# A gated graph layer on one Trainium2 core: edge lists made for 128 targets at once, a mark stored once and loaded twice by ScalarE's queue, constants on VectorE, an evenly paced opening

## The chip, the cores and the metric

The kernel runs on one core of one Trainium2 chip. The metric is the device time of one execution in microseconds (us). A core has five engines, each with a queue of its own that is worked off in order: TensorE (PE; its weight loads are shown as PEld), VectorE (DVE), ScalarE (ACT), GpSimd (POOL) and SyncE (SP). SP, ACT and POOL issue DMAs; what SP issues is shown as queue q1, what ACT issues as q10, POOL's indirect ones as q0. The engines wait for one another through semaphores. SBUF is the working memory, PSUM takes the results of matmuls.

## The reference

There are 16 batches of 1024 nodes with 256 features, and one adjacency matrix of 1024 x 1024 that is almost empty: under 1% of it is not zero. Cut to what matters:

```
pre_u  = h @ W1[:256];  pre_v = h @ W1[256:]
S[u,v] = sigmoid(relu(pre_u[u] + pre_v[v] + b1) @ W2 + b2)
a[v]   = sum over u of S[u,v] * adj[u,v] * h[u]
m[v]   = (sum over u of adj[u,v] * h[u]) * h[v]
out    = beta1*h + beta2*(a @ Wa + ba) + beta3*(m @ Wm + bm)
```

S is needed only where adj is not zero, so the kernel works on lists of edges.

## The kernel before, in words

**Blocks, windows, steps.** Targets v are cut into 8 blocks of 128, batches into 4 groups of 4. One *block* of the main loop is one pair of group and block of targets; there are 32, numbered k, the group g = k // 8. The 128 targets of a block are two *windows* of 64. A window's edges lie in 640 slots, 5 *steps* of 128 edges each. So the main loop has 320 steps n, ten to a block, and s is the step within the block.

**A step.** Five buffers hold fetched rows: `fetch` (line 402) gathers for 128 edges the rows of the sources from `table[g]`, four steps ahead, on POOL; a row holds pre_u and h of four batches. `expand` (413) multiplies the window's *mark*, a 0/1 matrix that says which target each slot belongs to, with the targets' rows X, and so spreads pre_v over the edges; it is called two steps ahead. `gate` (429) adds both on DVE (432), takes relu, the product with W2 and its sum (436), then the sigmoid on ACT (439), and ACT scales the one-hot rows with it (441). `aggregate` (443) sums on PE into 64 targets x 2 kinds (449). After five steps `window_end` (453) copies the sums (456), multiplies by h and transposes; after ten `block_end` (477) multiplies by Wm and Wa (489) and stores.

**The marks.** A mark is 128 x 640 floats: 64 targets, twice, since X holds a high part in one half of the partitions and a low part in the other (`halves`, 308). `lists` makes it, stores all 128 rows to `who` (219), and `load_mark` (409) loads it on SP's queue into one of two buffers, which the main loop calls at line 523, in step 3 and step 8 of each block, for the window whose first `expand` comes at the end of that same step. On SP's queue stand also the loads of `hT` (269) and `h_blk` (521), 512 KB each, and the stores of `tab` (292) and of the result (499).

**The lists.** For each of the 8 blocks of targets `lists` (162) loads 128 rows of the transposed adjacency matrix, finds up to 24 sources of each target with three rounds of max on DVE, counts them, finds by a matmul with a triangular constant at which slot each target begins (187 to 190), and then, window by window (208): marks the slots (215, 217), multiplies the mark with the rows R of the lists (222), copies the result by ACT (226), picks from it on DVE each edge's source (228 to 238) and its one-hot row (239), and gathers the 5 x 128 values of the matrix on POOL (243). It is a generator: each `yield` gives the turn back, and the caller sets the order. In the opening two lists run side by side; lists 4 to 7 are worked on in the main loop, one piece a step (537).

**The rows.** `rows` (272) makes one block of `table[g]` and pv, the targets' pre_v: four pieces of eight matmuls each, in the order u, v, u, v. The pieces share two PSUM buffers ("misc") with much else; u is copied by ACT (290), v by DVE (297) a step later. x itself is copied from DRAM to DRAM on ACT's queue (277). The 8 blocks of group 0 are made in the opening; in groups 0 to 2 the main loop makes those of the next group, 4 or 5 pieces a block.

**The order.** It is written out by hand: the order of the calls is the order in each engine's queue, and `after(step, f)` (259) puts f off to a later step. The opening is the loop of lines 356 to 369: 32 rounds, each with one piece of rows, one piece of each of the two lists that run, and in rounds 5 and on the halves of block 0. Then come the last weights (371 to 377), their scaling on DVE, the first marks and the first five fetches. After step 60, `count_rest` (248) takes on POOL a maximum over all partitions of how many edges did not fit, and DVE reads it at once (252). If any are left, a loop at the end works them off; with these inputs it has nothing to do.

**Constants.** POOL makes them with iota and memset (98 to 117), DVE compares (119 to 132), and POOL clears the five fetch buffers (334).

Of the kernel before, what the change touches and what calls it, by code (L numbers as in the profile page):

```python
# [14 lines left out]
P = 128  # L15
# [3 lines left out]
def kernel(  # L19
# [57 lines left out]
    who = [dram.tile([P, E], FP, name=f"who{w}") for w in range(NT * NW)]  # L77
# [20 lines left out]
    def iota(shape, pattern, base, step, name):  # L98
        t = const.tile(shape, FP, name=name)
        nc.gpsimd.iota(t, pattern=pattern, base=base, channel_multiplier=step,  # L100
                       allow_small_or_imprecise_dtypes=True)
        return t

    ident = const.tile([P, P], FP, name="ident")
    make_identity(nc, ident)
    ones = const.tile([P, 2], FP, name="ones")
    nc.vector.memset(ones[:, 0:1], 1.0)
    nc.vector.memset(ones[:, 1:2], -1.0)
    ukey = const.tile([P, N], FP, name="ukey")
# [3 lines left out]
    slot_of = iota([P, TW], [[P, TW]], 0, 1, "slot_of")  # L113
    nth = iota([P, S], [[1, S]], 0, 0, "nth")
    place = iota([P, W], [[1, W]], 0, 0, "place")
# [4 lines left out]
    nc.vector.tensor_scalar(mine, row_of.rearrange("p w t v -> p w (t v)"), row, None, ALU.is_equal)  # L120
    before = const.tile([P, NW, P], FP, name="before")
    nc.vector.tensor_scalar(before, row_of.rearrange("p w t v -> p w (t v)"), row, None, ALU.is_gt)
    swap = const.tile([P, P], FR, name="swap")
    far = iota([P, NW, W], [[-W, NW], [1, W]], W, 0, "far")
    nc.vector.tensor_scalar(swap, far.rearrange("p w v -> p (w v)"), row, None, ALU.is_equal)
    late = const.tile([P, 1], FP, name="late")
    nc.vector.tensor_scalar(late, row, float(W), None, ALU.is_ge)
    nc.vector.tensor_scalar(before[:, 1, :], before[:, 1, :], late, None, ALU.mult)

    ahead = const.tile([P, NW, W], FP, name="ahead")  # L130
    for w in range(NW):
        nc.vector.tensor_copy(ahead[:, w, :], before[:, w, :W])
# [29 lines left out]
    def lists(vt):  # L162
# [23 lines left out]
        for w in range(NW):  # L186
            nc.tensor.matmul(pw[:, w * RC:(w + 1) * RC], mine[:, w, :], R, start=True, stop=True)
# [485 lines left out]
```

## Time and profile before

| what | us |
|---|---|
| median of three runs (lowest, highest) | 1495.53 (1494.21, 1500.91) |
| the profiled execution | 1498.72 |
| its span in the trace | 1496.9 |
| busy in the span: PE | 1323.4 (88%) |
| busy in the span: VectorE | 1219.2 (81%) |
| busy in the span: ScalarE | 902.8 (60%) |
| busy in the span: GpSimd | 446.5 (30%) |

The profiled execution is one more run, and its own time is 1.8 us more than its span. A row of instructions reads: start, length, engine and line, operation, what is written <- what is read, shape, how many merged (x), and in brackets how long the engine had been idle before it and what ended that. "misc", "pc" and "acc" are PSUM buffers. A row of waits reads: who waited <- for whom, total, times, longest. A group's row has busy time and, behind it, the mean of one in ns. Matmuls are pipelined, so 8 of 0.39 us each that are shown as one row of 1.9 us are usual.

### The profile page before, as it was taken

How to read it: one execution, taken by the hardware profiler on the slowest of the kernel's cores; microseconds unless marked ns; L12 is line 12 of the kernel's file. 1: busy time of each engine (PE TensorE's matmuls, PEld its weight loads, DVE VectorE, ACT ScalarE, POOL GpSimd, SP SyncE). 2: the span in 40 equal slices, each digit the busy share in tenths (PEclk: the TensorE clock that was granted, in tenths of full speed). 3: DMA queues.
4: the chain of work that ended last, by engine and by line, in shares of the span. 5: the costliest groups of instructions: out<-in, count | busy, mean ns of one | idle time of the engine just before them, and what ended most of it. 6: DMA issues, size and time to landing. Idle time of an engine off the chain costs nothing.

```text
span 1496.9 us, 20978 instructions
## 1 busy us (share of the span) xinstructions
PE 1323.4 (88%) x6064; PEld 1118.5 (75%) x6064; DVE 1219.2 (81%) x3521; ACT 902.8 (60%) x2570; POOL 446.5 (30%) x420
## 2 busy tenths in 40 slices
PE   4776788878997979999997979988999999999987
PEld 3555677767786868887886868877888877778876
DVE  7774898879976968876986978867888999999984
ACT  1212564545665757755775757655777777778763
POOL 2543253334522222222222222222222333333320
PEclk8897999989998989999999999999999999999999
DMA  4447768767796879877987878877998898889982
GB/s 133 148 148 276 274 242 290 240 210 270 234 339 218 314 292 327 297 269 267 330 320 267 314 292 316 303 263 262 330 332 311 318 334 320 320 323 322 335 302 70
DMA packets 152396, 414.35 MB, mean 277 GB/s; under 512 B 17120, under 2 KB 100576, under 8 KB 116064
## 3 DMA queue, kind: packets, MB, share of 16 engines
q0 software_dynamic: 48640, 296.70, 55.2%
q1 hardware_dynamic: 84496, 97.86, 18.8%
q10 hardware_dynamic: 19136, 18.35, 3.9%
q8 instruction: 51, 0.84, 0.2%
q14 instruction: 73, 0.60, 0.1%
HBM read 412.99 MB, written 55.57 MB: 313 GB/s over the span
## 4 chain that ended last, share of the span: by engine, by line
PE 45%; DMA 12%; DVE 6%; issue 4%; ACT 1%; POOL 1%; POOLq 0%; SPq 0%; DVEq 0%
PE acc L449 21%; DMA mark<-who 10%; PE misc L489 9%; PE misc L287 7%; PE pc L418 6%; DVE t L436 3%; DVE t L432 2%; PE misc L471 2%; DMA fetched<-table,uidx 2%; POOL fetched L404 1%; PE misc L322 1%; ACT left L441 0%; DVE ev L460 0%; DVE low L314 0%; ACT LT L473 0%
## 5 line engine op out<-in xcount | busy, mean ns | idle before, releaser
L449 PE MATMUL acc<-fetched,left 128*128 128x256 f32 x2560 | 635.6, 393 | 30.5 <-ACT ev L456 18.8
L404 POOL DMA_INDIRECT fetched<-table,uidx x320 | 344.9, 1078 | 928.8 <-PE acc L449 777.5
L449 PEld LDWEIGHTS acc<-fetched,left 128*128 128x128 f32 x2560 | 500.2, 197 | 127.6 <-ACT ev L456 25.7
L436 DVE SCALAR_TENSOR_TENSOR t<-t,w_b 128x256 f32<-128x256 f32 x1280 | 470.3, 422 | 21.8 <-DVE t L432 0.9
L432 DVE TENSOR_TENSOR t<-fetched,pc 128x1024 f32<-128x1024 f32 x320 | 388.5, 1214 | 87.0 <-PE pc L418 62.6
L441 ACT ACTIVATE left<-left,gt 128x64 f32<-128x64 f32 x1280 | 340.9, 337 | 10.4
L418 PE MATMUL pc<-X,mark 128*128 128x512 f32 x640 | 248.3, 470 | 64.9 <-DMA mark<-who 52.6
L439 ACT ACTIVATE gt<-sc,b_b 128x4 f32<-128x4 f32 x320 | 95.9, 300 | 245.2 <-DVE t L436 243.5
L418 PEld LDWEIGHTS pc<-X,mark 128*128 128x128 f32 x640 | 119.8, 197 | 87.0 <-issue 44.3
L426 ACT ACTIVATE left<-onehot,val 128x256 f32<-128x256 bf16 x320 | 157.7, 493 | 5.3 <-DMA w_m<-in_Wm_dram 5.3
L287 PE MATMUL misc<-w_u,hT 128*128 128x256 f32 x512 | 132.3, 404 | 32.2 <-DVE pv L297 19.3
L287 PEld LDWEIGHTS misc<-w_u,hT 128*128 128x128 f32 x512 | 101.5, 202 | 50.8 <-DVE pv L297 21.8
L325 ACT CAST X<-misc 64x512 fp32r<-64x512 f32 x128 | 74.3, 580 | 106.4 <-PE misc L322 105.2
L489 PE MATMUL misc<-w_m,LT 128*128 128x256 f32 x512 | 135.3, 388 | 0.6 <-ACT X L325 0.3
L287 PE MATMUL misc<-w_v,hT 128*128 128x256 f32 x512 | 128.9, 397 | 5.7 <-ACT tab L290 4.1
L489 PE MATMUL misc<-w_a,LT 128*128 128x256 f32 x512 | 131.4, 379 | 0.0
L290 ACT COPY tab<-misc 128x512 f32<-128x512 f32 x64 | 37.5, 585 | 147.4 <-PE misc L287 139.0
L287 PEld LDWEIGHTS misc<-w_v,hT 128*128 128x128 f32 x512 | 99.9, 198 | 23.9 <-ACT tab L290 6.8
L489 PEld LDWEIGHTS misc<-w_m,LT 128*128 128x128 f32 x512 | 99.7, 196 | 16.3 <-ACT X L325 1.0
L243 POOL DMA_INDIRECT val<-in_adjT_dram,vidx x80 | 90.1, 1126 | 69.0 <-DVE none L202 24.0
L489 PEld LDWEIGHTS misc<-w_a,LT 128*128 128x128 f32 x512 | 97.5, 190 | 13.5
L436 DVE DVE_READ_ACCUMULATOR t<-t,w_b 128x1 f32 x1280 | 103.9, 81 | 0.0
(100 smaller groups left out, 933.6 us busy)
## 6 DMA issues: line engine op xcount, KB each, us to landing
mark<-who SPq DMA_DIRECT2D x65, 320.0 KB, 8.7
hT<-in_xT_dram SPq DMA_DIRECT2D x32, 512.0 KB, 11.5
table<-in_x_dram ACTq DMA_DIRECT2D x32, 512.0 KB, 8.5
table<-tab SPq DMA_DIRECT2D x32, 512.0 KB, 6.4
h_blk<-in_x_dram SPq DMA_DIRECT2D x32, 512.0 KB, 12.5
out_dram<-h_blk SPq DMA_DIRECT2D x32, 512.0 KB, 5.4
who<-made SPq DMA_DIRECT2D x16, 320.0 KB, 2.5
fetched<-table,uidx POOLq DMA_INDIRECT x320, 8.0
```

Of the source, the lines that this page charges most:

```text
L243: nc.gpsimd.indirect_dma_start(out=val[:, i, j:j + 1], out_offset=None, in_=adj_flat, in_offset=bass.IndirectOffsetOnAxis(ap=vidx[:, i, j: ...
L287: nc.tensor.matmul(p[:, bb * D:(bb + 1) * D], hT[:, 2 * h + bb, i, :], wt[:, i, :], start=(i == 0), stop=(i == DC - 1))
L325: nc.scalar.copy(X[s, w, c], pl[s])
L404: nc.gpsimd.indirect_dma_start(out=fetched[n % NF], out_offset=None, in_=table[g], in_offset=bass.IndirectOffsetOnAxis(ap=uidx[:, vt * NW ...
L418: nc.tensor.matmul(pcs[n][:, c], marks[n // TW][:, j * P:(j + 1) * P], cuts[k][:, w, c], start=True, stop=True)
L426: nc.scalar.activation(lefts[n][:, :, w, :], onehot[:, i, j, :].unsqueeze(1).to_broadcast([P, GB, W]), AF.Copy, scale=val[:, i, j:j + 1])
L432: nc.vector.tensor_tensor(t, fetched[n % NF][:, :GD].rearrange("p (b d) -> p b d", b=GB), pcs.pop(n).rearrange("p (b d) -> p b d", b=GB), ...
L436: nc.vector.scalar_tensor_tensor(t[:, b, :], t[:, b, :], 0.0, w2_b, ALU.max, ALU.mult, accum_out=sc[:, b:b + 1])
L439: nc.scalar.activation(gt, sc, AF.Sigmoid, bias=b2_b)
L441: nc.scalar.activation(lefts[n][:, b, 1 - w, :], lefts[n][:, b, w, :], AF.Copy, scale=gt[:, b:b + 1])
L449: nc.tensor.matmul(accs[n // TW][:, b, :], left[:, b].rearrange("p k v -> p (k v)"), f[:, GD + b * D:GD + (b + 1) * D], start=(j == 0 and ...
L489: nc.tensor.matmul(pz[:, bb * D:(bb + 1) * D], LTs[k][:, b * DC + c, i, :], wt[:, c, :], start=(i == 0 and c == 0), stop=(i == 1 and c == ...
```

## The change

- **Lists.** Both windows of a block go through one pass: one pair of marking operations for all 128 targets, five matmuls over 128 partitions with two masked copies of R side by side, one copy by ACT, one chain on DVE over 10 columns in place of 5, then all ten gathers. The start of each target's slots comes from one matmul, and DVE reads it from PSUM. A list has 9 pieces, where it had 12.
- **Mark.** `who` holds 64 rows; each load is two DMAs, one for each half of the partitions, issued by ACT. In the main loop they are issued in steps 4 and 9 of a block for the window after the next, behind that step's `gate` and `left_adj`.
- **Constants.** All are made on VectorE from one scan and a 32 x 32 transpose; POOL keeps the clearing of `val` and of the fetch buffers.
- **Rows.** The order is u, u, v, v; in group 0 both v pieces go to the PSUM tile of the sums and are copied in one operation.
- **Opening.** The 36 pieces of lists 0 to 3 are spread evenly over the 32 rounds, the two running lists by turns. The last weights are loaded eight rounds before the end, and are scaled after step 3 of the main loop.
- **Main loop.** No list piece in step 0 or in any step with s = 8. The all-reduce stays after step 60, DVE reads it twelve steps later.

```diff
-    who = [dram.tile([P, E], FP, name=f"who{w}") for w in range(NT * NW)]
+    who = [dram.tile([W, E], FP, name=f"who{w}") for w in range(NT * NW)]
...
-    slot = iota([P, E], [[1, E]], 0, 0, "slot")
...
-    row = iota([P, 1], [[0, 1]], 0, 1, "row")
-    row_of = iota([P, NW, 2, W], [[W, NW], [0, 2], [1, W]], 0, 0, "row_of")
-
-    mine = const.tile([P, NW, P], FP, name="mine")
-    nc.vector.tensor_scalar(mine, row_of.rearrange("p w t v -> p w (t v)"), row, None, ALU.is_equal)
...
+    upto = fixed([P, E], "upto")
+    nc.vector.tensor_scalar(upto, ukey[:, :E], -1.0, float(N), ALU.mult, ALU.add)
+    rows32 = fixed([P, 32], "rows32")
+    nc.vector.transpose(rows32, upto[:, :32])
+    row = rows32[:, 0:1]
...
+    nc.vector.tensor_scalar(ahead[:, :W], upto[:, :W], row, None, ALU.is_gt)
+    nc.vector.tensor_scalar(ahead[:, W:], upto[:, W:P], row, late, ALU.is_gt, ALU.mult)
...
+    slot, nth, place = upto, upto[:, :S], upto[:, :W]
@@ lists
         pw = aside(vt)
-        for w in range(NW):
-            nc.tensor.matmul(pw[:, w * RC:(w + 1) * RC], mine[:, w, :], R, start=True, stop=True)
-        for w in range(NW):
-            nc.tensor.matmul(pw[:, NW * RC + w:NW * RC + w + 1], before[:, w, :], R[:, 0:1], start=True, stop=True)
-        nc.tensor.matmul(pw[:, NW * RC + NW:NW * RC + NW + 1], ahead.rearrange("p w v -> p (w v)"), R[:, 0:1],
-                         start=True, stop=True)
+        nc.tensor.matmul(pw[:, 0:1], ahead, R[:, 0:1], start=True, stop=True)
         yield
-        Rw = wk.tile([P, NW * RC + NW + 1], FP, name="Rw", bufs=2)
-        nc.scalar.copy(Rw, pw[:, :NW * RC + NW + 1])
+        first = R[:, 1:2]
+        nc.vector.tensor_copy(first, pw[:, 0:1])
...
+        early = wk.tile([P, E], FP, name="early", bufs=1)
+        nc.vector.tensor_scalar(early, slot, R[:, 0:1], None, ALU.is_lt)
...
+        mark = big.tile([P, E], FP, name="made", bufs=2)
+        nc.vector.scalar_tensor_tensor(mark, slot, first, early, ALU.is_ge, ALU.mult)
...
-        for w in range(NW):
...
-            mark = big.tile([P, E], FR, name="made", bufs=1)
-            nc.vector.scalar_tensor_tensor(mark, slot, first, early, ALU.is_ge, ALU.mult)
-            yield
-            nc.sync.dma_start(who[i], mark.bitcast(FP))
-            pe = aside(vt)
-            for j in range(TW):
-                nc.tensor.matmul(pe[:, j * RC:(j + 1) * RC], mark[0:W, j * P:(j + 1) * P].bitcast(FP), Rv[0:W, :],
-                                 start=True, stop=True)
-            yield
...
+        yield
+        RR = wk.tile([P, NW, RC], FP, name="RR", bufs=2)
+        for w, mine in enumerate((soon, late)):
+            nc.vector.tensor_scalar(RR[:, w, :], R, mine, None, ALU.mult)
+            nc.sync.dma_start(who[vt * NW + w], mark[w * W:(w + 1) * W])
+        pe = aside(vt)
+        for j in range(TW):
+            nc.tensor.matmul(pe[:, j * NW * RC:(j + 1) * NW * RC], mark[:, j * P:(j + 1) * P],
+                             RR.rearrange("p w r -> p (w r)"), start=True, stop=True)
+        yield
+        M = NW * TW
+        L = wk.tile([P, M, RC], FP, name="L", bufs=2)
+        nc.scalar.copy(L.rearrange("p (w j) r -> p w j r", w=NW),
+                       pe[:, :M * RC].rearrange("p (j w r) -> p w j r", w=NW, r=RC))
...
+        yield
+        nc.vector.tensor_tensor(onehot[:, sl].rearrange("p w j v -> p (w j) v"),
...
+        for i in range(vt * NW, (vt + 1) * NW):
             for j in range(TW):
                 nc.gpsimd.indirect_dma_start(
...
@@ rows
+        for wt in (w_u, w_v):
+            for h in range(2):
+                c = slice(2 * h * D, (2 * h + 2) * D)
+                if wt is w_v and g == 0 and h == 0:
+                    both = psa.tile([P, GD], FP, name="acc")
+                p = both[:, c] if wt is w_v and g == 0 else small("p")
...
+                elif g:
+                    after(step + 1, lambda c=c, p=p: keep(c, p))
+                elif h == 1:
+                    after(step + 1, lambda both=both: keep(slice(0, GD), both))
@@ opening
-    while m < 0 or any(pair):
...
-        for i in range(2):
-            if pair[i] and not (m < 2 - 4 * NT and i == 1) and next(pair[i], 0) == 0:
+    OP = 4 * NT
+    for m in range(OP):
+        all_rows.send(m - OP - 10)
...
+        for _ in range((m + 1) * 9 * EARLY // OP - m * 9 * EARLY // OP):
+            i = at % 2 if pair[at % 2] else (at + 1) % 2
+            at += 1
+            if pair[i] and next(pair[i], 0) == 0:
...
+        if m == OP - 8:
+            w_a = load_weights(Wa, "w_a")
...
+    def scale_late():
...
+    after(3, scale_late)
@@ load_mark
         marks[q] = big.tile([P, E], FR, name="mark")
-        nc.sync.dma_start(marks[q].bitcast(FP), who[q % (NT * NW)])
+        src = who[q % (NT * NW)]
+        for h in range(2):
+            nc.scalar.dma_start(marks[q][h * W:(h + 1) * W].bitcast(FP), src)
@@ main loop
-        if n % TW == TW - 2 and n + TW < total:
-            load_mark(n // TW + 1)
...
+        if n % TW == TW - 1 and n // TW + 2 < total // TW:
+            load_mark(n // TW + 2)
...
-        if n < total:
+        if 0 < n < total and s != 8:
             next(more, None)
...
         if n == 60:
-            count_rest()
+            nc.gpsimd.partition_all_reduce(longest, rest, P, bass_isa.ReduceOp.max)
+            after(n + 12, count_rest)
```

More of the change, by code (lines that the diff above doesn't have):

```diff
@@ L6 @@
 from concourse._compat import with_exitstack
-from concourse.masks import make_identity
 FP = mybir.dt.float32
@@ L246, in lists @@
                     bounds_check=N * N - 1, oob_is_err=False)
+    longest = const.tile([P, NT], FP, name="longest")
     def count_rest():
-        longest = const.tile([P, NT], FP, name="longest")
-        nc.gpsimd.partition_all_reduce(longest, rest, P, bass_isa.ReduceOp.max)
         most = const.tile([P, 1], FP, name="most")
```

137 lines of the change are left out of this document (59 added, 78 removed).

## The prediction

> **What bounds the kernel now.** I read the table by stage first. I cut it at VectorE's add of line 432, which begins each edge step: 140.70 is step 0, and a block of 128 targets is ten steps. Columns: length, then busy time with instruction count of PE, PEld, DVE, ACT and POOL, then granted clock, DMA share and GB/s.
>
> ```profile
> 0.00:140.70 140.70, 91.80 (x390) 72.01 (x390) 88.83 (x215) 24.79 (x46) 59.38 (x64) 0.88 0.51 161
> 140.70:403.60 262.90, 221.47 (x978) 180.80 (x979) 226.59 (x669) 141.84 (x405) 96.20 (x84) 0.92 0.75 258
> 403.60:443.70 40.10, 39.19 (x187) 33.77 (x186) 34.34 (x102) 29.81 (x87) 14.56 (x15) 1.00 0.87 315
> 443.70:493.70 50.00, 41.67 (x184) 35.29 (x183) 34.02 (x103) 25.67 (x73) 11.80 (x11) 0.90 0.72 243
> 493.70:528.60 34.90, 34.90 (x169) 30.30 (x168) 32.68 (x96) 27.04 (x79) 11.15 (x10) 1.00 0.88 320
> 528.60:707.70 179.10, 163.31 (x736) 139.38 (x735) 135.95 (x394) 111.35 (x319) 42.24 (x40) 0.93 0.81 288
> 707.70:785.90 78.20, 77.90 (x375) 67.91 (x374) 68.38 (x197) 57.27 (x165) 21.57 (x20) 1.00 0.92 328
> 785.90:867.80 81.90, 74.25 (x350) 64.40 (x349) 66.76 (x195) 52.62 (x151) 21.64 (x20) 0.96 0.80 287
> 867.80:1046.70 178.90, 159.79 (x736) 137.06 (x735) 135.69 (x395) 111.47 (x319) 42.30 (x40) 0.96 0.80 288
> 1046.70:1197.30 150.60, 150.30 (x723) 131.19 (x722) 135.03 (x393) 109.89 (x316) 42.29 (x40) 1.00 0.91 323
> 1197.30:1437.80 240.50, 225.08 (x1054) 190.42 (x1053) 225.68 (x675) 185.86 (x540) 75.78 (x70) 0.99 0.89 321
> ```
>
> There are five stages. The opening (140.7) keeps PE and DVE each some two thirds busy, so neither bounds it alone. Blocks 0 to 4 (262.9), where four lists are still made, are nearest to DVE (226.6 busy). Blocks that make rows for the next group are bound by PE: at 707.7 two take 78.2 with PE busy for 77.9. The stages at 528.6 and 867.8 are four such blocks each, the same work as twice 78.2 = 156.4, yet take 179.1 and 178.9, with PE idle for 16 to 19 us. The last seven whole blocks are DVE's, 225.7 of 240.5. The idle time of PE is explained by the waits, then SyncE's issues in order of time, then the marks' DMAs.
>
> ```profile
> DVE t L432 <- PE pc L418: 62.6, 31, 8.1
> PE pc L418 <- DMA mark<-who: 52.6, 13, 8.0
> ```
>
> ```profile
> 528.41 0.38 SPq L521 DMA_DIRECT2D h_blk<-in_x_dram  x1
> 528.84 0.96 SPq L269 DMA_DIRECT2D hT<-in_xT_dram  x1
> 529.89 9.51 SPq L411 DMA_DIRECT2D mark<-who  x1
> ```
>
> ```profile
> L411 SPq DMA_DIRECT2D mark<-who x65: 319/373/11349, 125.9 to 1437.9; - x65
> ...
> DMA to landing us min/median/max: 3.6/8.7/22.4
> ```
>
> Line 418 spreads a window's marks, and DVE waits for line 418 in turn. An issue of a mark usually takes 0.37 us; behind a block's rows and an hT of 512 KB each it takes 9.5, and the landing stretches from 8.7 to as much as 22.4 us.
>
> **The change, part by part.**
>
> *Marks.* Line 523 asks for a window's mark in the very step whose end multiplies with it, through SyncE behind those big loads. The change asks four steps earlier (about 15 us at 78.2/20 = 3.9 us a step), through ScalarE. The buffer is free by then: its last reader is the spread two steps back, for which the gate just run has waited, so ScalarE waits for nothing. What goes is the excess over the undisturbed stages: 179.1 - 156.4 = 22.7; 178.9 - 156.4 = 22.5; and 81.9 against the same pair at the end of the next group (150.6 - 78.2 = 72.4), 9.5. Together **-55**. What is late next there is PE itself, as at 707.7 and 1046.7, where DMA already ran at 0.91 to 0.92. Bounds: -59 (with the marks of other blocks) to -15 (landings stay as long as the longest now).
>
> The Trainium skill, DMA: Bandwidth & Descriptors, section Rules for kernel authors, speaks against this part: two transfers to disjoint halves share the same engines, one of 128 partitions is better, and spreading over issuing engines saves only issue time. By it the load itself gets no faster; the trace agrees that issue time is much of the loss (9.5 us above), and the first rival below is what is left.
>
> *ScalarE's share.* Two issues a window, 128 in all.
>
> ```profile
> 117.98 0.56 ACTq L277 DMA_DIRECT2D table<-in_x_dram  x1
> ```
>
> ```profile
> ACT gt L439 <- DVE t L436: 45.6, 39, 1.9
> ```
>
> At 0.37 to 0.56 each that is 47 to 72 us of ScalarE. It lies ahead of the next gt, line 439; gt and, through it, PE's line 449 are queued behind. In the PE-bound blocks ScalarE is busy 110 of 150, so it is covered. In the last seven blocks gt still waited for DVE 39 times, 45.6 / 39 = 1.2 us each, which covers most pairs of 0.7 to 1.1. I charge **+2** (0 to +15, if half of the last windows and a few others pay a pair).
>
> *Opening.*
>
> ```profile
> 13.86 9.15 DVE L120 TENSOR_SCALAR mine<-row_of,row 128x256 f32<-128x256 f32 x1 [0.17 <-POOL row_of L100]
> ```
>
> ```profile
> L334 POOL MEMSET fetched<- 128x2048 f32 x5 | 8.8, 1796 | 0.0
> ```
>
> ```profile
> 29.45 3.78 PE L287 MATMUL misc<-w_u,hT 128*128 128x256 f32 x8 [10.67 <-DVE pv L297]
> ```
>
> ```profile
> 120.47 1.00 POOL L243 DMA_INDIRECT val<-in_adjT_dram,vidx  x1 [0.30 <-issue]
> 121.77 1.00 POOL L243 DMA_INDIRECT val<-in_adjT_dram,vidx  x1 [0.30 <-issue]
> 131.22 0.99 POOL L404 DMA_INDIRECT fetched<-table,uidx  x1 [8.45 <-issue]
> ```
>
> ```profile
> 125.50 0.32 SPq L292 DMA_DIRECT2D table<-tab  x1
> ```
>
> ```profile
> 140.72 1.22 DVE L432 TENSOR_TENSOR t<-fetched,pc 128x1024 f32<-128x1024 f32 x1 [3.99 <-DMA fetched<-table,uidx]
> ```
>
> One DVE constant of 128x256 stood for 9.15 us, as long as POOL's memsets; PE then stood for 10.7, since both small PSUM buffers waited for DVE. Without iotas POOL's memsets begin at once, so the new constants, all DVE's, stand beside them until about 9 to 10 and are done by about 13; now the list work resumes at 13.86 + 9.15 = 23.0.
>
> The Trainium skill, SBUF — State Buffer, section Who interferes with whom, makes this an exclusive lock: whoever issues second blocks. The trace agrees in the 9.15 above; were there no lock, the constants would be done some 6 us sooner.
>
> Each list's DVE work shrinks, and so do DVE's waits for it, shown here for blocks 0 to 4:
>
> ```profile
> 43.94 0.15 DVE L228 TENSOR_TENSOR s_of<-slot_of,L 128x5 f32<-128x5 f32 x1
> ...
> 45.76 0.48 DVE L239 TENSOR_TENSOR onehot<-place,L 128x320 bf16<-128x320 f32 x1
> ```
>
> ```profile
> 47.59 0.56 DVE L215 TENSOR_SCALAR early<-slot,Rw 128x640 f32<-128x640 f32 x1
> 48.24 0.88 DVE L217 SCALAR_TENSOR_TENSOR made<-slot,Rw,early 128x640 fp32r<-128x640 f32 x1
> ```
>
> ```profile
> DVE s_of L228 <- ACT L L226: 20.0, 8, 5.2
> DVE held L198 <- ACT Rw L194: 8.7, 4, 3.7
> ```
>
> One of two passes goes: 45.76 - 43.94 = 1.8 and 0.56 + 0.88 = 1.4, less some 0.6 for the wider operations and two masked copies of R: 2.6 a list. Of the 88.8 busy, 9.2 goes with the stuck constant, 4 x 2.6 = 10.4 with the lists, 1.8 is moved (below): 67 are left. Begun at 10, with four waits for ScalarE's L of 20.0 / 8 = 2.5 us each, DVE ends near 87; PE, with somewhat under its 91.8 of work, near 90. But the lists are now spread over all 32 pieces, so the third and fourth end with the last pieces: the indices of the third are ready about 7 us before the end, at 83, and POOL then has 20 gathers at 121.77 - 120.47 = 1.30, to 109, before the first fetch in its queue. Now the gathers ended at 122.8, ahead of the table. From fetch to first gate took 140.72 - 131.22 = 9.5, so the first gate comes at about 118: **-23**. Bounds: -39 (first gate at 102, if the gathers kept out of the way: last table store near 87, then 131.22 - 125.50 = 5.7, then 9.5) to -5 (the lists end 18 us later than I think).
>
> *Blocks 0 to 4.* DVE is idle 262.9 - 226.6 = 36.3. L is copied four times, not eight: -10; Rw is not copied by ScalarE at all: -8.7. DVE's work: -10.4 for the lists, +1.8 for the scaling of weights, which now runs after step 3 where it was hidden in the opening. Sum -27; the mark, and one list wait that goes with shorter queues, make it **-30**. What is late next is DVE. Ten gathers in a row (13 us) stand ahead of a fetch that has four steps of slack. Bounds: -15 to -40.
>
> *The all-reduce.*
>
> ```profile
> 460.06 0.40 POOL L250 PARTITION_ALL_REDUCE longest<-rest  x1 [9.65 <-issue]
> 460.65 1.25 POOL L404 DMA_INDIRECT fetched<-table,uidx  x1 [0.20 <-issue]
> ```
>
> ```profile
> fetched<-table,uidx POOLq DMA_INDIRECT x320, 8.0
> ```
>
> The block at 443.7 took 50.0; one like it is 72.4 - 34.9 = 37.5. DVE now waits for POOL; the change lets DVE read twelve steps later. But POOL's own 9.65 stays, and the fetch behind it, at 460.65, lands 8.0 later, at 468.7; its gate, five steps of 3.75 after 443.7, is due at 462.5. So 6.2 of the 12.5 stays: **-6** (-3 to -12).
>
> *The last window's mark* came late once more, in a block without other large loads:
>
> ```profile
> 1456.18 0.76 PE L418 MATMUL pc<-X,mark 128*128 128x512 f32 x2 [2.88 <-DMA mark<-who]
> ```
>
> **-2** of that (0 to -3).
>
> *Sum*: -55 + 2 - 23 - 30 - 6 - 2 = -114. The profiled execution took 1498.72 (span 1496.9 and 1.8 around it): 1385. It lies 0.2% above the median of 1495.53, less than any term here, and I leave that out.
>
> **The rivals.**
>
> *Marks stay late.* If the load is slow because all DMA is busy (0.92 at 707.7), and not because of its queue, a landing of 22.4 against 15 us of lead leaves 7.4 at some eight windows, with PE's slow restart some 45 of the 55: 1385 + 45 = 1430. For it: the share. Against: the stages with the highest share, 707.7 and 1046.7, lose nothing.
>
> *The opening isn't held by POOL.* If the gathers overlap the table's landing, the first gate comes at 102: 1385 - 16 = 1369. Against: POOL's queue is in order.
>
> *The opening gains little.* If DVE and PE, coupled step by step, end near 105, the gathers end at 124 and the first gate is at 134: 1401.
>
> *Slower: ScalarE is held in the issue as SyncE was.* One mechanism: the mark behind a table copy on ScalarE's queue blocks the engine itself, for 9.5 us as at 529.89, once in each of 24 row blocks: 24 x 9.5 = 228, so 1613. It decides from a mean of 114 / 24 = 4.8 us on. Against: SyncE was held behind two loads of 512 KB, here one copy stands ahead, and it was issued in 0.56.
>
> *It doesn't do what it says*: the marks are asked early, but a store or a buffer holds them to the old time. Then only the rest counts: 1440.
>
> **How the numbers follow.** The forecast with its own bounds 0.65; marks late 0.12; opening free 0.10; opening slow 0.07; no early marks 0.03; slower 0.03. The forecast's terms, two or three missing their mark together, reach 1345 to 1425; the late marks put the upper end at 1430; beyond lie the last two cases and the forecast's tails. Half a percent, 7 us, is about what a measurement of this kernel can tell from no change. All cases but the slower one are faster by more; for a sum of small failures I leave 0.02 at no change: faster 0.95, same 0.02, slower 0.03.
>
> **What would show it.** Right: no wait of line 418's matmul for a mark over 1 us; the four-block stages at 156 each; first gate near 118 with POOL's gathers running up to the first fetch; no 13 us wait of DVE for the all-reduce, but a fetch wait of some 6 us five steps on; ScalarE's issues near 0.4 us. Wrong: waits for marks in the same blocks as now, issues on ScalarE of several us, or a first gate after 130.

## The result and the profile after

The median after is 1400.57 us (four runs, 1396.24 to 1402.45), against 1498.10 before (four runs, 1494.21 to 1500.91): a ratio of 0.9347, 95% interval 0.9311 to 0.9382, so 6.5% faster. The forecast was 1385, with a range of 1345 to 1430. The profiled execution took 1396.24, with a span of 1394.4; that of before was 1496.9. TensorE's mean granted clock rose from 0.952 to 0.977. Ratios, here and below, leave out runs more than 1.5% above the fastest of the same kernel; that takes out four of the eleven runs of the kernel before that stood beside the second group of experiments.

The table by stage of the kernel after, cut at the same add (now line 441), with the same columns as before:

```profile
0.00:117.80 117.80, 71.69 (x318) 59.87 (x318) 70.03 (x163) 23.32 (x38) 60.00 (x55) 0.87 0.62 186
117.80:367.00 249.20, 206.98 (x907) 168.57 (x908) 217.33 (x625) 141.06 (x397) 101.26 (x88) 0.94 0.75 260
...
405.90:443.80 37.90, 37.90 (x184) 33.14 (x183) 33.97 (x99) 27.54 (x80) 11.21 (x11) 1.00 0.93 317
443.80:479.40 35.60, 35.30 (x169) 30.16 (x168) 33.61 (x100) 26.67 (x78) 11.17 (x10) 1.00 0.92 315
479.40:634.30 154.90, 154.22 (x735) 133.41 (x735) 134.97 (x394) 111.35 (x318) 44.19 (x40) 1.00 0.97 333
...
712.40:786.70 74.30, 73.23 (x351) 63.37 (x350) 67.51 (x195) 54.23 (x157) 20.88 (x20) 1.00 0.92 317
786.70:942.30 155.60, 154.35 (x736) 133.46 (x736) 135.03 (x395) 111.41 (x319) 43.50 (x40) 1.00 0.95 331
...
1094.10:1338.90 244.80, 224.39 (x1051) 187.07 (x1050) 225.48 (x675) 186.01 (x540) 81.24 (x70) 1.00 0.92 315
1338.90:1394.50 55.60, 42.65 (x200) 35.04 (x198) 35.02 (x101) 25.14 (x81) 8.13 (x7) 0.97 0.50 180
```

Subtracting each length from that of the same blocks before gives the balance:

| stage | before | after | gain | forecast |
|---|---|---|---|---|
| opening | 140.7 | 117.8 | 22.9 | 23 |
| blocks 0 to 4 | 262.9 | 249.2 | 13.7 | 30 |
| block 6 (all-reduce) | 50.0 | 37.9 | 12.1 | 6 |
| blocks 8 to 11, 14 to 15, 16 to 19 (marks) | 439.9 | 384.8 | 55.1 | 54.7 |
| last seven whole blocks | 240.5 | 244.8 | -4.3 | -2 |
| the last block and the end | 59.1 | 55.6 | 3.5 | 2 |
| the rest (blocks 5, 7, 12 to 13, 20 to 23) | 303.8 | 304.4 | -0.6 | 0 |
| all | 1496.9 | 1394.5 | 102.4 | 114 |

The four-block stages are now PE's throughout: 154.22 busy of 154.90. Blocks 0 to 4 are where the forecast was missed: DVE's work there fell from 226.6 to 217.3, but 31.9 of its 36.3 of idle time stayed. The marks' own view after (issues on ScalarE: shortest, median and longest in ns), and its landings:

```profile
L420 ACTq DMA_DIRECT2D mark<-who x128: 452/513/1231, 81.4 to 1339.9; - x128
...
DMA to landing us min/median/max: 2.9/7.7/12.5
```

No issue holds ScalarE for more than 1.23 us, where one held SyncE for 9.5 to 11.3. The longest landing, 12.5 us, is inside the four steps of lead. Line 427 (the spread, line 418 before) waits for a mark once, 3.1 us in the opening, where it costs nothing, and in no block.

The opening, in order of time: first POOL's gathers and fetches, then DVE's first add. The bracket says how long the engine had been idle and what ended it.

```profile
84.89 1.12 POOL L237 DMA_INDIRECT val<-in_adjT_dram,vidx  x1 [7.81 <-DVE s_of L219]
...
110.29 0.99 POOL L237 DMA_INDIRECT val<-in_adjT_dram,vidx  x1 [0.30 <-issue]
111.58 1.00 POOL L411 DMA_INDIRECT fetched<-table,uidx  x1 [0.30 <-issue]
```

```profile
117.77 1.22 DVE L441 TENSOR_TENSOR t<-fetched,pc 128x1024 f32<-128x1024 f32 x1 [28.33 <-DMA fetched<-table,uidx]
```

Twenty gathers run without a gap up to the first fetch, and DVE stands idle for 28.3 us, with its own work of the opening done: POOL's queue sets the end of the opening.

DVE's waits inside blocks 0 to 4 of the kernel after (total, times, longest; of the fetch's 31.8, the 28.3 just shown lie before the first add), and then POOL's all-reduce:

```profile
DVE t L441 <- DMA fetched<-table,uidx: 31.8, 2, 28.3
DVE s_of L219 <- ACT L L216: 17.1, 4, 5.3
DVE key L169 <- DMA key<-in_adjT_dram: 1.8, 1, 1.8
DVE pv L280 <- PE misc L291: 1.7, 2, 1.1
```

```profile
413.10 1.03 POOL L568 PARTITION_ALL_REDUCE longest<-rest  x1 [0.21 <-issue]
```

L is copied half as often and yet costs 17.1 of the former 20.0. All four waits lie in step 0 of a block (reads at 166.6, 220.3, 272.0 and 329.1). The last of them, with ScalarE's rows ahead of its copy:

```profile
325.53 0.59 ACT L294 COPY tab<-misc 128x512 f32<-128x512 f32 x1 [2.75 <-PE misc L291]
...
327.72 1.01 ACT L465 COPY ev<-acc 128x1024 f32<-128x1024 f32 x1
328.62 0.41 ACT L216 COPY L<-misc 128x290 f32<-128x290 f32 x1
```

```profile
329.06 0.18 DVE L219 TENSOR_TENSOR s_of<-slot_of,L 128x10 f32<-128x10 f32 x1 [5.31 <-ACT L L216]
```

A list has nine pieces and a block nine steps that take one, so each list meets the same step; for the copy of L that is the step in which ScalarE also copies the sums (ev).

POOL's wait of 9.65 us ahead of the all-reduce, which the forecast kept, is gone.

### The profile page after: what moved, and what is told of

It reads as the page before. It is cut to its first block, busy times and chain, and to the rows that moved or that the text cites. A ratio compares the mean times of both kernels' runs of the same rounds, so it can differ in the third digit from the quotient of the medians.

```text
span 1394.4 us, 20649 instructions
## 1 busy us (share of the span) xinstructions
PE 1268.1 (91%) x5920; PEld 1076.6 (77%) x5920; DVE 1189.4 (85%) x3424; ACT 901.2 (65%) x2554; POOL 453.9 (33%) x411
## 4 chain that ended last, share of the span: by engine, by line
issue 32%; DVE 27%; DMA 13%; PE 12%; POOL 11%; ACT 3%; POOLq 1%; SPq 0%; DVEq 0%; ACTq 0%
POOL fetched L411 11%; DMA fetched<-table,uidx 10%; DVE t L445 10%; DVE t L441 9%; PE acc L458 4%; PE misc L291 3%; PE misc L498 2%; ACT left L450 1%; DVE ev L469 1%; DMA key<-in_adjT_dram 1%; DVE R L173 1%; DVE h_blk L490 1%; DMA val<-in_adjT_dram,vidx 1%; PE pc L427 1%; DMA hT<-in_xT_dram 1%
## 5 line engine op out<-in xcount | busy, mean ns | idle before, releaser
L458 PE MATMUL acc<-fetched,left 128*128 128x256 f32 x2560 | 618.0, 385 | 38.8 <-ACT ev L465 19.5
L411 POOL DMA_INDIRECT fetched<-table,uidx x320 | 350.6, 1096 | 839.6 <-PE acc L458 703.9
L458 PEld LDWEIGHTS acc<-fetched,left 128*128 128x128 f32 x2560 | 486.4, 192 | 134.5 <-ACT left L450 33.4
L450 ACT ACTIVATE left<-left,gt 128x64 f32<-128x64 f32 x1280 | 340.9, 337 | 10.4
L427 PE MATMUL pc<-X,mark 128*128 128x512 f32 x640 | 244.1, 463 | 31.1 <-DVE t L441 28.0
L291 PE MATMUL misc<-w_u,hT 128*128 128x256 f32 x512 | 125.1, 390 | 11.7 <-DMA hT<-in_xT_dram 8.7
L291 PEld LDWEIGHTS misc<-w_u,hT 128*128 128x128 f32 x512 | 98.2, 195 | 26.5 <-issue 8.7
L498 PEld LDWEIGHTS misc<-w_m,LT 128*128 128x128 f32 x512 | 96.2, 192 | 27.1 <-DVE h_blk L504 8.4
L237 POOL DMA_INDIRECT val<-in_adjT_dram,vidx x80 | 92.6, 1158 | 67.9 <-DVE eq L221 36.3
L291 PE MATMUL misc<-w_v,hT 128*128 128x256 f32 x384 | 91.2, 380 | 2.0 <-ACT LT L483 1.7
L469 DVE TENSOR_TENSOR ev<-ev,h_blk 64x1024 f32<-64x1024 f32 x64 | 78.0, 1219 | 10.6 <-ACT ev L465 9.6
```

What stands on the lines that cost most here:

```text
L237: nc.gpsimd.indirect_dma_start(out=val[:, i, j:j + 1], out_offset=None, in_=adj_flat, in_offset=bass.IndirectOffsetOnAxis(ap=vidx[:, i, j: ...
L291: nc.tensor.matmul(p[:, bb * D:(bb + 1) * D], hT[:, 2 * h + bb, i, :], wt[:, i, :], start=(i == 0), stop=(i == DC - 1))
L411: nc.gpsimd.indirect_dma_start(out=fetched[n % NF], out_offset=None, in_=table[g], in_offset=bass.IndirectOffsetOnAxis(ap=uidx[:, vt * NW ...
L427: nc.tensor.matmul(pcs[n][:, c], marks[n // TW][:, j * P:(j + 1) * P], cuts[k][:, w, c], start=True, stop=True)
L450: nc.scalar.activation(lefts[n][:, b, 1 - w, :], lefts[n][:, b, w, :], AF.Copy, scale=gt[:, b:b + 1])
L458: nc.tensor.matmul(accs[n // TW][:, b, :], left[:, b].rearrange("p k v -> p (k v)"), f[:, GD + b * D:GD + (b + 1) * D], start=(j == 0 and ...
```

## The experiments

Theory after the result: the marks were late because of their place behind SyncE's large loads and because they were asked late; the opening is bound by POOL's gathers; blocks 0 to 4 kept their idle time because DVE reads ScalarE's L in the piece that asks for it. Rivals are named with each run. "Before" was run beside every group; its medians were 1504.22, 1503.29 and 1498.88, so kernels of different groups are compared by their ratio. In the second group (even pacing to one load a mark) it scattered from 1485.69 to 1519.87, and there the stages of the profiles carry more than the times.

**Marks alone.** The kernel before, with the marks' load moved four steps ahead onto ScalarE's queue, still one DMA of 128 rows:

```diff
-        nc.sync.dma_start(marks[q].bitcast(FP), who[q % (NT * NW)])
+        nc.scalar.dma_start(marks[q].bitcast(FP), who[q % (NT * NW)])
...
-        if n % TW == TW - 2 and n + TW < total:
-            load_mark(n // TW + 1)
...
+        if n % TW == TW - 1 and n // TW + 2 < total // TW:
+            load_mark(n // TW + 2)
```

> The kernel before with one part alone: a window's mark is loaded four steps earlier and by ScalarE's queue, still as one DMA of 128 stored rows. Theory (the marks' late landing is worth the whole excess of the disturbed stages): the stages that took 179.1, 81.9 and 178.9 us become 156, 74 and 156 as in the changed kernel, the rest stays, so 1498 - 56 = 1442 us. Rival (most of that gain came with the other parts, from shorter lists or an earlier opening): less than 20 us, 1478 or more.

Measured: 1444.70 (1442.97 to 1445.87), ratio 0.9603, interval 0.9542 to 0.9663. Its table by stage, the three mark stages and the last seven whole blocks:

```profile
534.90:690.20 155.30, 153.96 (x735) 133.47 (x734) 134.97 (x394) 111.38 (x318) 42.54 (x40) 1.00 0.93 332
768.40:840.80 72.40, 72.40 (x350) 63.27 (x349) 66.78 (x195) 52.63 (x151) 21.37 (x20) 1.00 0.91 324
840.80:995.40 154.60, 153.98 (x736) 133.68 (x735) 135.21 (x394) 111.48 (x319) 43.67 (x40) 1.00 0.93 334
1146.00:1387.60 241.60, 224.60 (x1054) 189.04 (x1053) 225.22 (x673) 186.10 (x540) 77.83 (x70) 0.99 0.89 319
```

The three stages, 57.6 us shorter together, are as short as in the kernel after, so the marks' term is the marks' alone. Two further rows of this kernel, one of PE at the start and one of POOL in block 6:

```profile
145.99 2.08 PE L418 MATMUL pc<-X,mark 128*128 128x512 f32 x4 [14.72 <-DMA mark<-who]
```

```profile
467.33 0.40 POOL L250 PARTITION_ALL_REDUCE longest<-rest  x1 [10.00 <-issue]
```

The first mark, now on ScalarE's queue, came late, and cost some 6 us (first gate 147.3 against 140.7). The wait ahead of the all-reduce is there as before: early marks don't remove it.

**Engine or place.** The kernel after, with the early loads issued by SyncE:

```diff
-            nc.scalar.dma_start(marks[q][h * W:(h + 1) * W].bitcast(FP), src)
+            nc.sync.dma_start(marks[q][h * W:(h + 1) * W].bitcast(FP), src)
```

> The changed kernel with its early marks issued by SyncE in place of ScalarE. Theory (what counts is that the load stands ahead of the block's big loads in the order of its queue, not which engine issues it): 1398 to 1404 us, no wait for a mark over 2 us; the last seven blocks, at 244.8 us now and 240.5 before, tell what ScalarE's issues cost: back to 241 if they are the cause. Rival (SyncE's queue itself is what is slow): marks land up to 20 us after their issue as before, and 20 to 40 us of waits come back, 1420 to 1440.

Measured: 1398.22 (1394.06 to 1403.14), ratio 0.9288 (0.9228 to 0.9349): not to be told from the kernel after. The same step on SyncE does as well: the three mark stages take 154.3, 72.6 and 156.4, and past the opening PE waits for a mark once, for 1.2 us. The last seven whole blocks, with ScalarE free of every mark:

```profile
1097.60:1343.90 246.30, 227.41 (x1053) 191.34 (x1052) 225.14 (x673) 186.08 (x541) 77.25 (x70) 0.98 0.90 313
```

246.3 is no shorter than 244.8, so the tail doesn't pay for ScalarE's issue time, which is what the forecast's +2 charged.

**The same engine, late.** The kernel after, with the load put back to the old step, still on ScalarE:

```diff
+        if n % TW == TW - 2 and 1 < n // TW + 1 < total // TW:
+            load_mark(n // TW + 1)
...
-        if n % TW == TW - 1 and n // TW + 2 < total // TW:
-            load_mark(n // TW + 2)
```

> The changed kernel with the marks issued by ScalarE, but in the step whose end needs them, as the kernel before has it in its program. Theory (a queue that computes can't run ahead of its program, SyncE's could): each of 62 windows pays the landing of 7.7 us less some 3 us of the step that are left, about 5 us, so 1400 + 62 x 5 = 1710 us. Rival (the queue alone is the cure): 1400 to 1420.

Measured: 1677.44 (1666.24 to 1684.87), ratio 1.1129 (1.1045 to 1.1214). From its view of waits:

```profile
PE pc L427 <- DMA mark<-who: 220.1, 48, 9.3
```

48 of 64 windows wait 4.6 us each. These 220.1 us are most of the 288.6 by which this profile is longer than that of the kernel after; what the rest is made of wasn't followed (the mean granted clock fell from 0.977 to 0.911). The issues themselves stay short (median 0.51, longest 1.43 us), so ScalarE isn't held; it comes to the issue behind its own work. SyncE, which computes nothing, had run ahead of its place in the program: in the undisturbed stage at 707.7 of the kernel before it issued the two marks of a block at 716.18 and 722.52, while the steps that call for them began at 720.75 and 738.78. That lead is gone here. Of the two changes to the marks, the four steps are what counts; with the new engine and without them, the changed kernel is 11% slower than the kernel before.

**The wait ahead of the all-reduce.** The kernel after, with one unused iota at its very end:

```diff
+    junk = const.tile([P, 1], FP, name="junk")
+    nc.gpsimd.iota(junk, pattern=[[0, 1]], base=0, channel_multiplier=1, allow_small_or_imprecise_dtypes=True)
```

> The changed kernel with one iota of 128 x 1 on GpSimd added behind all its work; the result is used by nothing. Theory (the code of the all-reduce stays loaded from one execution to the next, and it was the iotas that displaced it): GpSimd again idles about 9.7 us before the all-reduce, though nothing stands before it in this execution, and some 9 to 11 us before the iota at the end. Rival (the all-reduce's code is loaded at each start, before the first instruction): no wait before the all-reduce, only before the iota.

Measured, one run: 1410.30. POOL's rows at the all-reduce and at the iota, then the row of block 6 in the table by stage:

```profile
427.65 0.44 POOL L568 PARTITION_ALL_REDUCE longest<-rest  x1 [10.67 <-issue]
428.29 1.87 POOL L411 DMA_INDIRECT fetched<-table,uidx  x1 [0.20 <-issue]
...
1383.99 0.14 POOL L572 IOTA junk<- 128x1 f32 x1 [9.09 <-issue]
```

```profile
410.00:454.90 44.90, 41.43 (x184) 34.98 (x183) 33.66 (x99) 27.64 (x80) 11.57 (x11) 0.92 0.77 271
```

No iota precedes the all-reduce in the execution, and still POOL waits 10.67 us ahead of it, and 9.09 ahead of the iota. The kernel before, where the iotas come first, shows the other half: POOL stands about as long ahead of its first iota.

```profile
12.13 0.66 POOL L100 IOTA slot<- 128x640 f32 x1 [11.20 <-issue]
```

The reading that fits all kernels is that what ran last in one execution is what the next one finds: with an iota anywhere in the program, the two kinds replace one another in every execution; without one (the kernel after), the all-reduce finds its code in place. The trace shows the waits and not what is loaded in them. Block 6 then takes 44.9, the 44 of the forecast: its step from a wait of 9.65 us to a block of 44 was right, its assumption that the wait stays was not.

**Even pacing alone.** The kernel after, with one piece of each of the two running lists every round, as before:

```diff
-        for _ in range((m + 1) * 9 * EARLY // OP - m * 9 * EARLY // OP):
-            i = at % 2 if pair[at % 2] else (at + 1) % 2
-            at += 1
-            if pair[i] and next(pair[i], 0) == 0:
+        for i in range(2):
+            if pair[i] and not (m < 2 and i == 1) and next(pair[i], 0) == 0:
```

> The changed kernel with the opening paced as before: each round takes a piece of both running lists, so the lists end about two thirds through. Theory (the opening's end is set by GpSimd, which has 20 gathers of 1.30 us between the last lists and the first fetch): the gathers end by about 96, before or with the table's landing, and the first gate comes at 100 to 104 in place of 117.8; the whole 14 to 17 us faster, 1383 to 1387. Rival (even pacing is what lets VectorE and TensorE run side by side): rows are held up by lists early on, the last piece of rows ends 10 us later or more, and the first gate stays at 112 to 120.

Measured: 1413.69 (1411.34 to 1422.01), ratio 0.9455 (0.9392 to 0.9517). POOL's rows around its first fetch:

```profile
102.28 1.00 POOL L237 DMA_INDIRECT val<-in_adjT_dram,vidx  x1 [0.30 <-issue]
123.66 1.00 POOL L409 DMA_INDIRECT fetched<-table,uidx  x1 [20.38 <-DMA table<-tab]
```

The expectation failed and its rival held in kind: the gathers do end early, but the fetch then waits 20.4 us for the table, since the rows end later (the last store of the table is issued at 118.00, where the kernel after issues it at 81.97). The first gate is at 131.8, 14 us behind that of the kernel after and later than the rival's 112 to 120 as well. In this opening DVE stands once for 16.1 us, and ScalarE twice for 14.0 together, for a releaser that the trace doesn't name; why the crowded order slows the rows so much stays open.

**Gathers out of the way.** The kernel after, with the gathers of lists 2 to 7 put off and issued two behind each step's fetch:

```diff
+                if vt < 2:
+                    gather()
+                else:
+                    later.append(gather)
...
+            for _ in range(2):
+                if later:
+                    later.pop(0)()
```

> The changed kernel with the gathers of lists 2 to 7 put off: two of them behind each step's fetch in the main loop, so that none stands before the first fetch but those of lists 0 and 1. Theory (GpSimd's queue sets the opening's end): first fetch at about 88, when the table has landed (last store 81.97 and 5.7), first gate at 94 to 97, 21 to 24 us earlier, with nothing lost later since a step has 1.3 + 2.6 = 3.9 us of GpSimd's work: 1376 to 1381 us. Rival (the wait is only moved: the fetches behind the put-off gathers come late in the first blocks): half of it is given back in blocks 0 to 4, 1388 to 1392.

Measured: 1380.79 (1375.60 to 1382.52), ratio 0.9222 (0.9168 to 0.9277). POOL's first fetch, and the first two stages:

```profile
89.61 0.99 POOL L418 DMA_INDIRECT fetched<-table,uidx  x1 [12.83 <-DMA table<-tab]
```

```profile
0.00:98.20 98.20, 72.57 (x318) 60.32 (x318) 72.04 (x162) 23.20 (x38) 38.17 (x35) 0.94 0.75 225
98.20:347.80 249.60, 206.11 (x902) 166.88 (x903) 217.93 (x625) 140.66 (x396) 118.25 (x108) 0.94 0.78 259
```

The fetch now waits for the table and no longer for gathers, and the first gate comes 19.6 us earlier. That is at 98.2, somewhat behind the 94 to 97 expected: from the first fetch to it took 8.6 us, where the kernel after took 6.2. This shows POOL's queue as the bound of the opening. Blocks 0 to 4 stay at 249.6 (249.2 before this edit), with twenty gathers more in them and none in a row of ten; so nothing is lost there, and the rows of ten that the forecast let pass are unlikely to have cost much.

**L copied a step earlier.** The kernel after, with one more yield between ScalarE's copy and DVE's reading of it:

```diff
+        if vt >= EARLY:
+            yield
```

> The changed kernel with one more yield in lists 4 to 7, between ScalarE's copy of L and VectorE's use of it. Theory (blocks 0 to 4 lost what I had counted as gain because VectorE waits 17.1 us for that copy, which stands in ScalarE's queue behind the step's other work, in step 0 also behind the copy of the sums): these waits go to 3 us or less, blocks 0 to 4 take 235 to 240 in place of 249.2, the whole 1388 to 1392. Rival (TensorE is what comes next in those steps, so the wait only changes its place): blocks 0 to 4 stay within 4 us of 249.

Measured: 1393.62 (1391.11 to 1395.32), ratio 0.9301 (0.9246 to 0.9357). Blocks 0 to 4 and DVE's longest waits in them (the fetch's 28.0 is the opening's):

```profile
118.00:364.10 246.10, 205.52 (x904) 169.74 (x905) 217.70 (x627) 142.34 (x399) 97.14 (x89) 0.93 0.77 267
```

```profile
DVE t L443 <- DMA fetched<-table,uidx: 28.4, 2, 28.0
DVE t L443 <- remote: 7.5, 1, 7.5
DVE pv L282 <- PE misc L293: 5.7, 5, 3.5
DVE key L169 <- issue: 4.3, 1, 4.3
DVE key L169 <- DMA key<-in_adjT_dram: 1.7, 1, 1.7
```

All 17.1 us of waits for L are gone and the stage is 3.1 shorter: new waits stand in their place, for the next list's key, for PE's rows and once for something the trace names only as remote. The 235 to 240 expected of the theory failed; the length is within the rival's 4 us of 249, though PE is only one of the new waits. The time can't be told from that of the kernel after (the intervals overlap). The yield does a second thing: it gives a list ten pieces for the nine steps of a block, so that the copies of L leave step 0 from the second of these lists on. The run doesn't separate the two.

**One load a mark.** The kernel after, with a window's 64 rows stored twice and loaded by one DMA of 128 rows:

```diff
-            nc.sync.dma_start(who[vt * NW + w], mark[w * W:(w + 1) * W])
+            for h in range(2):
+                nc.sync.dma_start(who[vt * NW + w][h * W:(h + 1) * W], mark[w * W:(w + 1) * W])
...
-        for h in range(2):
-            nc.scalar.dma_start(marks[q][h * W:(h + 1) * W].bitcast(FP), src)
+        nc.scalar.dma_start(marks[q].bitcast(FP), src)
```

> The changed kernel with each mark stored twice (two stores of 64 rows) and loaded by one DMA of 128 rows, by ScalarE as before. The last seven blocks took 240.5 before, 241.6 with early marks in one DMA, 244.8 here and 246.3 with the two DMAs on SyncE. Theory (two DMAs of 64 rows cost more than one of 128, whoever issues them): 241 to 242 in the last seven blocks, 3 us less in the whole, maybe some more in the blocks with rows. Rival (it is the issue on a computing engine, or chance): 244 to 246 again.

Measured: 1392.46 (1387.26 to 1395.49), ratio 0.9292 (0.9249 to 0.9335), which overlaps that of the kernel after. The stage it aims at, the last seven whole blocks, and DVE's wait for fetched rows there, here and then in the kernel after:

```profile
1094.10:1335.40 241.30, 225.75 (x1054) 190.16 (x1053) 225.19 (x673) 186.00 (x541) 77.48 (x70) 0.99 0.89 320
```

```profile
DVE t L441 <- DMA fetched<-table,uidx: 9.9, 7, 2.0
```

```profile
DVE t L441 <- DMA fetched<-table,uidx: 12.6, 11, 1.9
```

241.3 is what the kernel before (240.5) and the one with early marks in one piece (241.6) take; with two DMAs of 64 rows the stage took 244.8 and 246.3. The other kernels settle that this isn't chance: in the six with one load a mark (three of them below) the stage takes 239.1 to 241.7, in the six with two early loads 243.6 to 246.3. So the tail's 4.3 us come from halving the loads, and reach DVE in part through later fetched rows (waits of 12.6 in place of 9.9). The Trainium skill, DMA: Bandwidth & Descriptors, section Rules for kernel authors, advises one transfer over 128 partitions in place of two over disjoint halves; these stages agree.

**Together.** Spread gathers and one load; then also the earlier copy of L; then also the next list's key loaded behind the third maximum of the list before it:

```diff
+        if EARLY <= vt < NT - 1:
+            load_key(vt + 1)
         yield
         pw = aside(vt)
```

> The changed kernel with two edits at once: the gathers of lists 2 to 7 are put off and issued two behind each step's fetch, and a mark's window is stored twice and loaded by one DMA of 128 rows. Each took time off by itself: spreading 1400.6 to 1380.8, one load 1400.6 to 1392.5 (its last seven whole blocks 244.8 to 241.3). Theory: they act in different stages, the opening and the last blocks, so the gains add: first gate at 98 to 99, last seven blocks 241 to 242, time 1372 to 1378. Rival: the second store of each mark delays the table's stores in the opening, now that the gathers no longer cover it: first gate past 102 and 1380 or more.

> As the kernel with spread gathers and one load, and a yield behind ScalarE's copy of L for lists 4 to 7, so that DVE reads it one step later. Theory: as alone (1400.6 to 1393.6, and blocks 0 to 4 from 249.2 to 246.1), the waits of DVE for L go, about 14 us in blocks 0 to 4 of the kernel with spread gathers, but only some 3 to 7 us of it reaches the end, because the next late input takes its place (the key's load, ScalarE's tab copy): blocks 0 to 4 take 243 to 247, time 3 to 7 below the kernel without the yield. Rival: with the gathers' crowd on POOL gone nothing takes the place of the L waits: blocks 0 to 4 at 236 to 240 and 10 us or more below.

> As the kernel with spread gathers, one load and the earlier copy of L, and the next list's 128 rows of the adjacency matrix are loaded several pieces ahead (behind the third maximum of the list before it) instead of one piece ahead. Theory: what is left idle in blocks 0 to 4 is a row of single late inputs, and the key's load is one of them, 4.3 and 1.7 us in the kernel with the earlier copy alone: blocks 0 to 4 shorten by 2 to 6 us and the time by the same. Rival: the idle time moves to the next input again and the length stays within 2 us; then no single wait sets this stage but the order in which DVE, ScalarE and PE hand pieces to one another, and the 217 us of DVE work there are not reachable by moving one of them.

Measured: 1373.74 (ratio 0.9177, 0.9135 to 0.9220), 1365.92 (0.9119, 0.9075 to 0.9163) and 1365.33 (0.9110, 0.9066 to 0.9154). Blocks 0 to 4 of the three, in this order:

```profile
98.00:346.20 248.20, 207.66 (x905) 168.75 (x906) 218.04 (x627) 141.36 (x397) 117.24 (x108) 0.93 0.77 267
```

```profile
100.20:341.80 241.60, 205.49 (x901) 170.10 (x902) 217.77 (x626) 140.69 (x394) 112.69 (x101) 0.93 0.80 274
```

```profile
99.40:337.40 238.00, 205.68 (x901) 170.29 (x902) 217.63 (x627) 140.32 (x394) 110.67 (x101) 0.92 0.81 278
```

The two gains of the first add, as expected (1372 to 1378; first gate at 98.0, last seven blocks 240.4). The later reading of L takes 6.6 off blocks 0 to 4 here, where it took 3.1 off the kernel after, and 7.8 off the median, with intervals that overlap. That lies between the two expectations, a little beyond the theory's 3 to 7 and 243 to 247 and short of the rival's 10 and 236 to 240. The earlier key takes another 3.6 off the stage, within the theory's 2 to 6 and about the 3.5 that this DVE wait lasted:

```profile
DVE key L171 <- DMA key<-in_adjT_dram: 3.5, 1, 3.5
```

That last gain is seen in the profile alone; the medians, 0.6 apart, can't tell. It is also not far above chance: in the kernel after and the four whose edits leave this stage's lists and gathers alone it took 249.2 to 251.8. DVE's work is 217 to 218 us in all three. So the stage's idle time looks like a row of single late inputs, of which a removal can pay in part only, since the next late input takes some of its place. After these three edits 20.4 us of idle time (238.0 less 217.6) are left.

## Why the prediction held, and where its sum was 11 us short

*Marks, -55:* measured 55.1, and shown alone by the first run. The rival that they stay late because all DMA is busy is out: at a share of 0.97 the stage at 479.4 has no such wait. The rival that ScalarE is held in its issues is out as well (1.23 us at most); what would have made the kernel slower is ScalarE with the old lead. That the load would be held to its old time, the rival at 1440, is out with the 55.1. One price was loose from the start: eight windows of 7.4 us are 59 us before any slow restart, not 45, so the late marks would have come out at 1444 or more.

*Opening, -23:* the first gate came at 117.8, forecast 118. Two parts of the way missed and cancelled: the third list's indices were ready at 84.9 rather than 83, so the first fetch was at 111.6 rather than 109, while from there to the first gate took 6.2 and not 9.5. The mechanism, gathers ahead of the first fetch, is shown by the run that moves them: 98.2. The rival with the first gate at 102 is what happens when they are moved, and only then; the one with DVE and PE late, at 134, didn't come (the old pacing gives 131.8, but there the fetch waits for the table). On DVE's constants the step was wrong. It let them stand beside POOL's memsets until 9 or 10 and end at 13; they ended at 8.4:

```profile
3.25 1.47 DVE L108 TENSOR_SCALAR upto<-ukey 128x640 f32<-128x640 f32 x1
...
6.47 1.92 DVE L128 TENSOR_SCALAR swap<-upto,rows 128x64 fp32r<-128x64 f32 x2
6.67 1.78 DVE L130 TENSOR_SCALAR ident<-upto,rows 128x128 f32<-128x128 f32 x1
8.38 1.21 DVE L169 SCALAR_TENSOR_TENSOR key<-key,ukey 128x1024 f32<-128x1024 f32 x1
```

It cost the sum nothing, since the end of the opening hung on POOL.

*Blocks 0 to 4, -30:* this is the step that failed, "L is copied four times, not eight: -10". DVE's work fell by 9.3 (226.6 to 217.3), as the -10.4 and +1.8 had it, and the 8.7 for Rw went. But the four waits left for L took 4.3 us each, not 2.5, so 2.9 went and not 10. DVE reads L in the piece that asks for it, and in step 0 of a block ScalarE has gt, left and the copy of the sums ahead of it, and in most of them a tab. The mean of the old waits was carried over to a new place in the queues. The second half of the error is that waits were subtracted from the length one by one. Rw's 8.7 and L's 2.9 make 11.6, yet DVE's idle time fell by 4.4 only: waits for fetched rows (3.5), the key (1.8) and PE (1.7 and 1.3) came in. The run with the later reading of L shows the same, 17.1 us of waits gone for 3.1. The 16 us by which this stage missed are thus explained in kind, but not to the last of them: 20.4 of idle time is left in the best version, and the waits named remote stay unnamed.

*All-reduce, -6:* the gain was 12.1, since POOL's own wait went too. The forecast took the wait as a property of the operation; in these runs it comes only where iota and all-reduce stand in one program.

*ScalarE's issues, +2:* measured 4.3 in the last seven blocks, of another cause: two loads of 64 rows in place of one of 128. The forecast had put the extra load's cost on ScalarE alone.

*The last window's mark, -2:* the end gained 3.5.

Together: 16 too much for blocks 0 to 4 and 2 too little charged to the tail, against 6 and 1.5 too little for the all-reduce and the end, and about 1 in the rest. That is the 11 us between 1385 and the profiled 1396.24; the median lies another 4.3 above.

## What to carry to other kernels

A wait for another engine's copy is priced by what stands in that engine's queue at the new place, not by the mean of the old waits. In a stage with many small waits, count a removed wait as a gain only after looking at which input comes next. A load's place in the program is not yet its time: an engine that computes nothing can ask for it well ahead, one that computes gets to it only behind its own work. A transfer that is late is first asked for earlier; which engine asks matters only if it reaches the issue late or is held there. And an engine's queue that is in order (POOL's gathers here) is worth sorting by who needs the result first: that was worth some 20 us with no work removed.

## What the runs showed of the hardware

The code of POOL's iota and all-reduce seems to replace one another and to stay from one execution to the next: POOL stood 9.65, 10.00 and 10.67 us ahead of the all-reduce in the three kernels that hold an iota, 11.20 and 10.03 ahead of the first iota in the two that open with iotas, 9.09 ahead of a closing iota, and 0.20 to 0.21 us ahead of the all-reduce in the ten kernels without one. The Trainium skill, GPSIMD Engine Reference, section 2.1 Instruction dispatch, gives about 6 us for the first call to a freshly loaded kernel; the waits here are one and a half times to nearly twice as long.

Beside POOL's memsets no row of DVE's constants took more than 1.92 us in the kernel after, about the length of one memset (1.88, from 9.38 for five), where a single constant had been held 9.15 us across five memsets in the kernel before; the trace doesn't show why the two differ.
